# Moving a quarter-layer of key projections from one attention stage into an earlier one

## The chip, the cores and the metric

The kernel runs on one core of a Trainium2 chip. The metric is device time in microseconds (us), the median of several runs: 2410.93 us before the change (three runs, 2410.16 to 2412.91). Five engines work from queues of their own: TensorE (PE, matmuls; PEld is its loading of the stationary operand), VectorE (DVE), ScalarE (ACT), GpSimd (POOL) and SyncE (SP, which here only issues DMA transfers). Each engine takes its instructions in a fixed order and waits on semaphores.

## The reference, cut to what matters

Two transformer layers act on x of 4 batches x 512 tokens x 512 features. Every sublayer has the form `x = x + layernorm(f(layernorm(x)))`.

- Layer 0 attention: 32 heads of width 16, one shared key and value head, ALiBi bias, causal.
- Layer 0 FFN: one 512 x 512 product with dequantized weights and a bias.
- Layer 1 attention: 32 query heads of width 128, 8 key and value heads (groups g = 0..7, four query heads each), causal. Keys and values pass through a low-rank product; half of each key's coordinates are rotated by position (RoPE).
- Layer 1 FFN: a gated FFN with ternary octonion weights.

What the change touches is the key of layer 1:

```python
k_r0 = hidden_states @ Wkr.T             # the rotated coordinates
k = k * cos + _rotate_half(k) * sin
c_kv = hidden_states @ Wdk.T
k_c = c_kv @ Wupk.T                      # the other coordinates
key_full = zeros.at[..., NOPE_IDX].set(k_c).at[..., ROPE_IDX].set(k_r)
scores = jnp.einsum('bhqd,bhkd->bhqk', q, k) * scale
```

The kernel merges both key matrices into one 512 x 128 weight per group, so that the key of one (group, batch) is one product of 128 x 512 by 512 x 512, followed by a rotation whose tables are 1 and 0 on the coordinates that are not rotated.

## The kernel before

**Precision.** Matmuls run in fp32r. To keep fp32 accuracy every operand is held as a high and a low part, and a product is three matmuls per 128-wide slice of the contraction: high x high, high x low, low x high (`mm3`, and `mm3_gen`, which yields between slices). A product over 512 features takes 12 matmuls, each with a weight load of its own.

**Stages.** Layer 0 attention, and woven into it the layer 0 FFN and what layer 1 needs of x; then layer 1 attention (`phase_b`); then layer 1 FFN (class `C`).

**Layer 0 attention** is class `A1`. `run` loops over 128 steps u, one per batch, head group and block, plus 13 more to drain. In each step, four sub-steps issue the score matmuls whose row maxima DVE takes (`max_tile`, L426 and L430), and, 12 steps behind, the score matmuls whose exponentials ACT takes (`exp_tile`, L467 and L470) and the products with the values (`pv`, L483). `self.exped` counts blocks of exponentials that were issued, `self.ended` finished batches. Everything else in this stage is a Python generator in `self.gens`. `slot()` advances each of them by one yield, and it is called twice per sub-step, so eight times per step u. `hop(n)` yields n times. That is how the source order is paced; a planner in the framework, which simulates times, then sets the order on each engine.

The generators are: the query projections (`projections`), the loads of queries into QS (`loads`), the transposition of the outputs (`o_piece`) and of the maxima (`max_end`), the weight products of layer 1 (`A2.products`, which leaves the merged key weights in DRAM as `wk_d`), and two streams of posts. A post (`A2.post`) takes one tile of 128 tokens after its batch has ended: output projection, layernorm, residual, the layer 0 FFN, layernorm, residual, then the normalized x of layer 1 in transposed high and low parts. It stores these to DRAM as `xt_d` (L826) and goes on to project the values of layer 1, stored as `v_d` (L840). The last batch's four posts run side by side after the attention.

Most generators take their PSUM from the pool `mm` of two banks. A counter with two tokens (`Tok`, `self.tok`) guards it in the source: who finds no token yields and tries again.

**Layer 1 attention** is `phase_b`: 32 units u, each one group g = u // 4 and one batch b = u % 4. A unit has 16 places p (four blocks of 128 queries by four heads). While unit u computes scores, softmax, transposed probabilities, products with the values and the output projection, it also projects the queries of unit u + 1 (`qproj`, four times) and its keys (`kproj`, once, at the place j == 3 of block 0). `kproj` is 12 matmuls of 512 columns and `rope`: three DVE products out of PSUM (L859, L861, L862), a sum on POOL (L863), the rounded high part on ACT (L864) and the low part on POOL (L865); for the first unit DVE takes the place of POOL. `load_x`, `load_kv` and `load_wk` bring x, the values and the key weights from DRAM through SP's queue, x two units ahead, the values nearly one.

**Memory.** In layer 0 the key weights of layer 0 (wk_h, wk_l) are read only until the last batch's keys are projected, and the key tiles KS0 and KS1 until their batches' last exponentials; KS3 lies in another pool. The zeros that a load of QS copies came from KS0.

Of the kernel before, what the change touches and what calls it, by code (L numbers as in the profile page):

```python
# [9 lines left out]
F32 = mybir.dt.float32  # L10
# [10 lines left out]
B, S, D = 4, 512, 512  # L21
NT = B * S // 128
# [193 lines left out]
class A1:  # L216
# [40 lines left out]
    def setup(self):  # L257
        nc, aps, P = self.nc, self.aps, self.wqp
        self.wk_h = self.wp.tile([128, KC, 128], F32R, name="wk_h")
        self.wk_l = self.wp.tile([128, KC, 128], F32R, name="wk_l")  # L260
# [15 lines left out]
    def setup_consts(self):  # L276
# [4 lines left out]
        def ks(i):  # L281
            k = (self.kp if i == B - 1 else wp).tile([128, 2, 512], F32R, name=f"KS{i}")
            nc.gpsimd.memset(f(k), 0.0)
            for two in range(2):
                last = nc.gpsimd.dma_start(k[48 + 64 * two:64 + 64 * two, two], aps["c_ks"])
            self.KS.append(k)
            return last

        last = ks(0)
        with self.tc.issue_after(last.ins):  # L290
# [7 lines left out]
            self.zero = f(self.KS[0][64:68, 0, :])  # L298
# [293 lines left out]
class A2:  # L592
# [3 lines left out]
    def __init__(self, tc, nc, c, aps, a1, o_d, x2_d, xt_d, v_d, wk_d, wv_d, P):  # L596
        self.tc, self.nc, self.c, self.aps, self.a1 = tc, nc, c, aps, a1
        self.o_d, self.x2_d, self.xt_d, self.v_d = o_d, x2_d, xt_d, v_d
# [184 lines left out]
    def post(self, b, t):  # L783
# [41 lines left out]
        for i, e in enumerate((xh, xl)):  # L825
            out.dma_start(self.xt_d[i][b][:, :, bass.ts(t, 128)], f(e))  # L826
        while self.wv is None:
            yield
# [15 lines left out]

    def posts(self):

        todo = [(b, t) for b in range(B - 1) for t in range(4)]

        def stream():
            while todo:  # L850
                yield from self.post(*todo.pop(0))

        return [stream(), stream()] + [self.post(B - 1, t) for t in range(4)]
# [14 lines left out]
def phase_b(tc, nc, c, aps, xt_d, wk_d, v_d, acc, xp, P, tern, tail):  # L868

    if True:  # L870
# [43 lines left out]
        def load_kv(u):  # L914
# [6 lines left out]
            KV[u] = ts  # L921

# [7 lines left out]
        def kproj(u):  # L930
            wh, wl = W["k", u // 4]
# [96 lines left out]
        load_wk(0)  # L1028
# [4 lines left out]
        load_kv(0)  # L1033
        for j in range(4):
# [219 lines left out]
def mega(tc, nc, aps, out):  # L1254
    with ExitStack() as top:
# [16 lines left out]
        v_d = [[dp.tile([8, 128, 4, 128], F32, name=f"v{i}{b}") for b in range(B)] for i in range(2)]  # L1272
        wk_d = [dp.tile([8, 128, KC, 128], F32, name=f"wk_d{i}") for i in range(2)]
# [4 lines left out]
        with ExitStack() as e1:  # L1278
# [8 lines left out]
            a2 = A2(tc, nc, c, aps, a1, o_d, x2_d, xt_d, v_d, wk_d, wv_d, P1)  # L1287
            start = {4: [a2.weights()], 5: [a2.load_wv()], 6: a2.posts()}
            a1.run(lambda u: start.get(u, []))
        with ExitStack() as e3:  # L1290
# [4 lines left out]
            with ExitStack() as eb:  # L1295
                phase_b(tc, nc, c, aps, xt_d, wk_d, v_d, acc, xp, pools(eb), tern,
# [98 lines left out]
```

## Time and profile before

| what | value |
|---|---|
| median of three runs | 2410.93 us |
| profiled execution, whole | 2413.31 us |
| its span, first to last instruction | 2411.6 us |
| mean granted TensorE clock over the span | 0.981 |
| PE / DVE / POOL / ACT busy | 2301.8 / 1573.0 / 1190.3 / 1076.9 us |
| first and last maxima of layer 0 (L426) | 40 and 582 us |
| last exponential matmul of layer 0 (L467) | 667 us |
| first matmul of layer 1's projections | 728 us |
| last product with the values in layer 1 | 2147 us |
| DMA traffic over the span | 241.54 MB, mean 100 GB/s |

How to read it. Times in the trace count from the first instruction of the profiled execution. A group row names line, engine, operation, `out<-in` by the program's tile names, the shape and the count. A row of the timeline has start, duration, engine and line; in brackets stands the idle time before it and what ended it. A row of a table by stretch gives the stretch, its length, and for each engine the busy time and the number of instructions, then the granted TensorE clock, the mean busy share of the 16 DMA engines and the GB/s moved. Matmuls are pipelined and the ends of their records are modelled, so a busy PE is not PE at its peak: the distance between starts tells more.

### The profile page before, as it was taken

What the parts mean: (1) busy time and instruction counts of PE and PEld (TensorE: products, weight loads), DVE (VectorE), ACT (ScalarE), POOL (GpSimd) and SP (SyncE); (2) the same over time, 40 slices, a digit from 0 to 9 for tenths busy, and PEclk for the clock granted to TensorE, in tenths of its full rate; (3) what the DMA queues carried; (4) which work ended last, traced back from release to release, by engine and by line L of the source; (5) the groups of instructions that cost most, each with busy time, mean ns of one, the idle gap of its engine ahead of it and who ended that gap; (6) DMA issues with size and microseconds to landing.
All of it is one profiled execution on the core that took longest, in us unless ns stands there. A gap on an engine that the chain in (4) does not pass through costs nothing.

```text
span 2411.6 us, 35873 instructions
## 1 busy us (share of the span) xinstructions
PE 2301.8 (95%) x11606; PEld 1794.2 (74%) x11606; DVE 1573.0 (65%) x4631; ACT 1076.9 (45%) x2404; POOL 1190.3 (49%) x1387
## 2 busy tenths in 40 slices
PE   6899889988889999999999999999999999999998
PEld 4566455555557788888888888888888888878886
DVE  7766656555356777777777767777777778764443
ACT  3555445545543344444444444444444445453332
POOL 3323333434343676566566566666656667522221
PEclk8899899999999999999999999999999999999999
DMA  8845434343367432233122222232222222041000
GB/s 183 238 145 181 98 92 111 89 106 110 94 188 207 135 103 75 88 101 102 66 88 105 70 88 97 79 106 70 88 97 79 91 85 79 14 127 57 31 27 18
DMA packets 158558, 241.54 MB, mean 100 GB/s; under 512 B 26738, under 2 KB 91506, under 8 KB 149540
## 3 DMA queue, kind: packets, MB, share of 16 engines
q1 hardware_dynamic: 141748, 202.42, 27.9%
q0 software_dynamic: 14768, 35.92, 5.3%
q8 instruction: 93, 1.52, 0.3%
q10 hardware_dynamic: 1856, 0.92, 0.2%
q14 instruction: 93, 0.76, 0.1%
HBM read 183.17 MB, written 63.92 MB: 102 GB/s over the span
## 4 chain that ended last, share of the span: by engine, by line
PE 84%; issue 4%; DMA 4%; DVE 3%; POOL 2%; ACT 2%; SPq 1%; ACTq 0%; POOLq 0%; DVEq 0%
PE mm L182 11%; PE mm L184 11%; PE mm L183 11%; PE pt L989 6%; PE mm L159 3%; PE pt L467 3%; PE po L483 3%; PE po L1002 3%; PE po L1003 3%; PE mm L161 3%; PE po L1004 3%; PE mm L160 3%; PE ps L969 3%; PE ps L970 3%; PE ps L971 3%
## 5 line engine op out<-in xcount | busy, mean ns | idle before, releaser
L980 POOL TENSOR_TENSOR s<-s,r 128x384 f32<-128x384 f32 (+3 forms) x512 | 359.6, 722 | 130.0 <-DVE r L979 119.7
L977 ACT ACTIVATE s<-s,mn 128x384 f32<-128x384 f32 (+3 forms) x512 | 286.0, 560 | 223.8 <-DVE mn L973 215.9
L863 POOL TENSOR_TENSOR rp_a<-rp_a,rp_b 128x512 f32<-128x512 f32 x155 | 200.3, 1292 | 262.3 <-DVE rp_b L862 247.5
L992 ACT CAST ph<-pt 128x512 fp32r<-128x512 f32 x320 | 181.7, 586 | 295.5 <-PE pt L989 287.8
L430 DVE CUSTOM_DVE_ANT_0 jk<-ps,mask 128x384 bf16<-128x384 f32 (+3 forms) x512 | 227.5, 483 | 81.2 <-PE ps L426 72.1
L993 DVE TENSOR_TENSOR pl<-pt,ph 128x512 fp32r<-128x512 f32 x320 | 216.5, 686 | 43.4 <-ACT ph L992 40.4
L973 DVE CUSTOM_DVE_ANT_0 s<-ps,mask 128x384 f32<-128x384 f32 (+2 forms) x384 | 203.1, 552 | 37.7 <-PE ps L971 19.5
L470 ACT ACTIVATE pe<-pt 128x512 f32<-128x512 f32 x307 | 174.4, 600 | 97.0 <-PE pt L467 92.7
L989 PE MATMUL pt<-ident,s 128*128 128x128 f32 x1280 | 214.1, 272 | 0.7 <-POOL s L980 0.5
L182 PE MATMUL mm<-xh,w_h 128*128 128x512 f32 x512 | 205.4, 401 | 2.1 <-DVE rp_b L862 1.9
L182 PE MATMUL mm<-w_h,oh 128*128 128x512 f32 x512 | 203.7, 398 | 0.7 <-ACT oh L1008 0.7
L184 PE MATMUL mm<-xh,w_l 128*128 128x512 f32 x512 | 203.6, 398 | 0.0
L183 PE MATMUL mm<-xl,w_h 128*128 128x512 f32 x512 | 202.1, 395 | 0.0
L183 PE MATMUL mm<-w_l,oh 128*128 128x512 f32 x512 | 201.7, 394 | 0.0
L184 PE MATMUL mm<-w_h,ol 128*128 128x512 f32 x512 | 200.3, 391 | 0.0
L989 PEld LDWEIGHTS pt<-ident,s 128*128 128x128 f32 x1280 | 164.7, 140 | 46.1 <-POOL s L980 1.1
L865 POOL TENSOR_TENSOR ql<-rp_a,qh 128x512 fp32r<-128x512 f32 x124 | 160.5, 1294 | 49.6 <-ACT qh L864 49.6
L472 POOL TENSOR_SCALAR_AFFINE_SELECT pe<-pe 128x512 f32<-128x512 f32 x128 | 82.5, 647 | 195.7 <-ACT pe L470 195.1
L859 DVE TENSOR_TENSOR rp_a<-mm,cosq 128x512 f32<-128x512 f32 x128 | 88.4, 691 | 119.6 <-PE mm L184 94.3
L426 PE MATMUL ps<-KS,QS 128*128 128x256 f32 (+2 forms) x384 | 132.7, 384 | 19.2 <-DVE mn L430 18.7
L108 POOL TENSOR_TENSOR ln_rs<-ln_ve,mhalf 128x1 f32<-128x1 f32 x112 | 63.8, 575 | 173.0 <-DVE ln_ve L106 145.5
L1008 ACT CAST oh<-po 128x512 fp32r<-128x512 f32 x128 | 74.5, 582 | 166.1 <-PE po L1004 165.9
(359 smaller groups left out, 5872.5 us busy)
## 6 DMA issues: line engine op xcount, KB each, us to landing
xh<-xt SPq DMA_DIRECT2D x32, 1024.0 KB
xl<-xt SPq DMA_DIRECT2D x32, 1024.0 KB
vh<-v SPq DMA_DIRECT2D x32, 256.0 KB
vl<-v SPq DMA_DIRECT2D x32, 256.0 KB
raw<-in_a_wo SPq DMA_DIRECT2D x32, 256.0 KB
w_h<-in_a_wo POOLq DMA_DIRECT2D x32, 256.0 KB, 3.2
m_d<-t_d SPq DMA_DIRECT2D x192, 42.5 KB
QS<-qh_d SPq DMA_DIRECT2D x62, 128.0 KB
```

Source lines behind the costliest of these rows:

```text
L182: nc.tensor.matmul(ps, lh(k), rh(k), start=(j == 0), stop=False)
L183: nc.tensor.matmul(ps, lh(k), rl(k), start=False, stop=False)
L184: nc.tensor.matmul(ps, ll(k), rh(k), start=False, stop=(j == n - 1))
L430: nc.vector.tensor_tensor_reduce(out=jk[:, :nk], in0=p, in1=self.c.mask[:, 384 - 128 * qb:512], scale=-1.0, scalar=3e38, op0=ALU.add, op1= ...
L470: nc.scalar.activation(e, ps, AF.Exp)
L863: eng.tensor_tensor(a, a, r, ALU.add)
L973: nc.vector.tensor_tensor_reduce(out=s[:, :nk], in0=ps[:, :nk], in1=mask, scale=-1.0, scalar=3e38, op0=ALU.add, op1=ALU.min, accum_out=mn)
L977: nc.scalar.activation(s[:, :nk], s[:, :nk], AF.Exp, bias=mn, scale=-1.0, accum_out=l)
L980: nc.gpsimd.tensor_tensor(s[:, :nk], s[:, :nk], r.to_broadcast([128, nk]), ALU.mult)
L989: nc.tensor.transpose(pt[:, j], PS[u, qb, j][:, bass.ts(kb, 128)], c.ident)
L992: nc.scalar.copy(ph, pt)
L993: nc.vector.tensor_tensor(pl, pt, f(ph), ALU.subtract)
```

## The change

A new generator, `keys`, joins layer 0 attention beside the two post streams. Once 64 blocks of exponentials have been issued (so that KS0 and KS1 are done with) and all four tiles of batch 0 have stored `xt_d`, it projects and rotates layer 1's keys of batches 0 and 1, in 32 items of (batch, half of 256 tokens, group). For each half it loads x from `xt_d` into tiles of the layer 0 front (tags xn and x). For each group it loads the key weights into the tiles that held layer 0's, yields five times, takes a token, issues 12 matmuls of 256 columns (one yield after each three), rotates with three DVE products, and a POOL sum, an ACT copy and a POOL subtraction, and stores both parts to a new DRAM tensor `k_d`. The rotation tables lie in KS0's place, two output buffers in KS1's.

In layer 1, `kproj` returns at once for units of batch 0 and 1, and `load_kv` loads those units' keys from `k_d`. The key weights are still loaded for every group, since batches 2 and 3 need them; the first such load moves behind the first loads of x, tables and values. The zeros for QS come from KS3.

```diff
+    def keys(self):
+        a1, nc, c, aps = self.a1, self.nc, self.c, self.aps
+        half = lambda tag, bufs: a1.tmp.tile([128, 2, 256], F32R, name="k_x", tag=tag, bufs=bufs)
+        while a1.exped < 64 or self.split[0] < 4:
+            yield
+        tab = a1.wp.tile([128, 2, S], F32, name="k_tab", tag="KS0")
+        for i, n in enumerate(("c_cosk", "c_sink")):
+            nc.sync.dma_start(tab[:, i], aps[n])
+        out = a1.wp.tile([128, 2, 2, 256], F32R, name="k_out", tag="KS1")
+        n = 0
+        for b in range(KB):
+            while self.split[b] < 4:
+                yield
+            for hf in range(2):
+                ts = bass.ts(hf, 256)
+                x = [half("xn", 3), half("xn", 3), half("xn", 3), half("x", 2)]
+                for i, t in enumerate(x):
+                    nc.sync.dma_start(f(t), self.xt_d[i // 2][b][:, 2 * (i % 2):2 * (i % 2) + 2, ts])
+                rp = f(half("x", 2))
+                for g in range(8):
+                    w = [a1.wp.tile([128, 512], F32R, name="k_w" + e, tag="wk_" + e) for e in "hl"]
+                    for i in range(2):
+                        nc.sync.dma_start(f(w[i]), self.wk_d[i][g])
+                    yield from hop(5)
+                    yield from self.tok.take()
+                    ps = self.mmp.tile([128, 256], F32, name="mm", tag="mm")
+                    yield from mm3_gen(nc, ps, lambda k: w[0][:, bass.ts(k, 128)],
+                                       lambda k: w[1][:, bass.ts(k, 128)],
+                                       lambda k: x[k // 2][:, k % 2], lambda k: x[2 + k // 2][:, k % 2],
+                                       range(KC), hops=1)
+                    cos, sin = tab[:, 0, ts], tab[:, 1, ts]
+                    nc.vector.tensor_tensor(rp[:, 0], ps, cos, ALU.mult)
+                    yield from hop(1)
+                    nc.vector.tensor_tensor(rp[0:64, 1], ps[64:128], sin[0:64], ALU.mult)
+                    nc.vector.tensor_tensor(rp[64:128, 1], ps[0:64], sin[64:128], ALU.mult)
+                    self.tok.give()
+                    nc.gpsimd.tensor_tensor(rp[:, 0], rp[:, 0], rp[:, 1], ALU.add)
+                    yield from hop(1)
+                    o = out[:, n % 2]
+                    n += 1
+                    nc.scalar.copy(o[:, 0], rp[:, 0])
+                    nc.gpsimd.tensor_tensor(o[:, 1], rp[:, 0], f(o[:, 0]), ALU.subtract)
+                    nc.sync.dma_start(self.k_d[b][g][:, :, ts], f(o))
+                    yield
...
-        return [stream(), stream()] + [self.post(B - 1, t) for t in range(4)]
+        return [stream(), stream(), self.keys()] + [self.post(B - 1, t) for t in range(4)]
...
         def load_kv(u):
...
+            if b < KB:
+                K[u] = kvp.tile([128, 2, S], F32R, name="k", tag="k")
+                nc.sync.dma_start(f(K[u]), k_d[b][g])
...
         def kproj(u):
+            if u % 4 < KB:
+                return
...
-        load_wk(0)
         cosk, sink, cosq, sinq = (cp.tile([128, S], F32, name=n) for n in ("cosk", "sink", "cosq", "sinq"))
         load_x(0)
...
         load_kv(0)
+        load_wk(0)
...
-            self.zero = f(self.KS[0][64:68, 0, :])
+            self.zero = f(self.KS[B - 1][64:68, 0, :])
```

`KB` is 2, `self.split[b]` counts the tiles of batch b whose `xt_d` stores were issued.

More of the change, by code (lines that the diff above doesn't have):

```diff
@@ L21 @@
 B, S, D = 4, 512, 512
+KB = 2
 NT = B * S // 128
@@ L258, in setup @@
         nc, aps, P = self.nc, self.aps, self.wqp
-        self.wk_h = self.wp.tile([128, KC, 128], F32R, name="wk_h")
-        self.wk_l = self.wp.tile([128, KC, 128], F32R, name="wk_l")
+        self.wk_h = self.wp.tile([128, KC, 128], F32R, name="wk_h", tag="wk_h")
+        self.wk_l = self.wp.tile([128, KC, 128], F32R, name="wk_l", tag="wk_l")
         self.wq_h = P.tile([128, KC, 512], F32R, name="wq_h", tag="wq_h")
@@ L281, in ks @@
         def ks(i):
-            k = (self.kp if i == B - 1 else wp).tile([128, 2, 512], F32R, name=f"KS{i}")
+            k = (self.kp if i == B - 1 else wp).tile([128, 2, 512], F32R, name=f"KS{i}", tag=f"KS{i}")
             nc.gpsimd.memset(f(k), 0.0)
@@ L592, with __init__ @@
 class A2:
-    def __init__(self, tc, nc, c, aps, a1, o_d, x2_d, xt_d, v_d, wk_d, wv_d, P):
+    def __init__(self, tc, nc, c, aps, a1, o_d, x2_d, xt_d, v_d, k_d, wk_d, wv_d, P):
         self.tc, self.nc, self.c, self.aps, self.a1 = tc, nc, c, aps, a1
+        self.k_d, self.split = k_d, [0] * B
         self.o_d, self.x2_d, self.xt_d, self.v_d = o_d, x2_d, xt_d, v_d
@@ L826, in post @@
             out.dma_start(self.xt_d[i][b][:, :, bass.ts(t, 128)], f(e))
+        self.split[b] += 1
         while self.wv is None:
@@ L865, in rope, with phase_b @@
     eng.tensor_tensor(dst_l, a, f(dst_h), ALU.subtract)
-def phase_b(tc, nc, c, aps, xt_d, wk_d, v_d, acc, xp, P, tern, tail):
+def phase_b(tc, nc, c, aps, xt_d, wk_d, v_d, k_d, acc, xp, P, tern, tail):
     if True:
@@ L1272, in mega @@
         v_d = [[dp.tile([8, 128, 4, 128], F32, name=f"v{i}{b}") for b in range(B)] for i in range(2)]
+        k_d = [dp.tile([8, 128, 2, S], F32, name=f"k_d{b}") for b in range(KB)]
         wk_d = [dp.tile([8, 128, KC, 128], F32, name=f"wk_d{i}") for i in range(2)]
@@ L1286, in mega @@
                 tern.store(c)
-            a2 = A2(tc, nc, c, aps, a1, o_d, x2_d, xt_d, v_d, wk_d, wv_d, P1)
+            a2 = A2(tc, nc, c, aps, a1, o_d, x2_d, xt_d, v_d, k_d, wk_d, wv_d, P1)
             start = {4: [a2.weights()], 5: [a2.load_wv()], 6: a2.posts()}
@@ L1295, in mega @@
             with ExitStack() as eb:
-                phase_b(tc, nc, c, aps, xt_d, wk_d, v_d, acc, xp, pools(eb), tern,
+                phase_b(tc, nc, c, aps, xt_d, wk_d, v_d, k_d, acc, xp, pools(eb), tern,
                         pc.front(0))
```

## The prediction

> **What bounds the kernel now.** I read the page first: one profiled execution, 2413.3 us in all with a span of 2411.6 us, 2.4 us above the median of the runs (2410.93). TensorE (PE) is busy nearly throughout and carries 84% of the chain that ended last.
>
> ```profile
> span 2411.6 us, 35873 instructions
> PE 2301.8 (95%) x11606; PEld 1794.2 (74%) x11606; DVE 1573.0 (65%) x4631; ACT 1076.9 (45%) x2404; POOL 1190.3 (49%) x1387
> PE 84%; issue 4%; DMA 4%; DVE 3%; POOL 2%; ACT 2%; SPq 1%; ACTq 0%; POOLq 0%; DVEq 0%
> ```
>
> Busy PE hides a difference, since a matmul's recorded duration overlaps the next one's. So I read starts: in time order, PE inside layer 1 attention, with all 12 matmuls of one key projection (L182 to L184, wk_h and wk_l).
>
> ```profile
> 1107.58 0.40 PE L182 MATMUL mm<-xh,wk_h 128*128 128x512 f32 x1
> 1107.81 0.40 PE L183 MATMUL mm<-xl,wk_h 128*128 128x512 f32 x1
> 1108.05 0.39 PE L184 MATMUL mm<-xh,wk_l 128*128 128x512 f32 x1
> ...
> 1110.25 0.39 PE L184 MATMUL mm<-xh,wk_l 128*128 128x512 f32 x1
> 1110.48 0.28 PE L964 MATMUL ps<-k,qh 128*128 128x256 f32 x1
> ...
> 1110.94 0.28 PE L969 MATMUL ps<-k,qh 128*128 128x256 f32 x1
> 1111.06 0.28 PE L970 MATMUL ps<-k,qh 128*128 128x256 f32 x1
> 1111.18 0.28 PE L971 MATMUL ps<-k,ql 128*128 128x256 f32 x1
> ```
>
> Starts follow each other every 0.23 us with 512 columns and every 0.12 us with 256, though each is recorded as 0.40 and 0.28. In layer 1 there is no hole in this row of starts. In layer 0 there are many. I cut layer 0 attention where each block of eight steps u begins its maxima (every 24th matmul of L426), and took each block's busy time; the last row is one unit of layer 1.
>
> ```profile
> core 0: us, PE busy (x) PEld busy (x) DVE busy (x) ACT busy (x) POOL busy (x), PEclk, DMA share, GB/s
> 136.10:174.40 38.30, 38.16 (x212) 27.48 (x211) 21.54 (x81) 17.57 (x33) 4.63 (x8) 1.00 0.36 119
> 237.40:264.70 27.30, 21.21 (x118) 10.66 (x117) 16.50 (x70) 12.12 (x23) 10.33 (x13) 0.81 0.68 177
> 414.10:438.80 24.70, 24.70 (x152) 15.16 (x151) 17.20 (x79) 16.00 (x29) 10.37 (x16) 1.00 0.34 55
> 438.80:482.40 43.60, 38.50 (x212) 25.15 (x211) 26.56 (x104) 21.52 (x39) 18.39 (x27) 1.00 0.42 106
> 1100.00:1143.00 43.00, 43.00 (x223) 36.08 (x222) 32.34 (x89) 20.55 (x54) 30.05 (x34) 1.00 0.29 93
> ```
>
> The same attention work takes 24.7 to 43.6 us, by what the generators add beside it. The first of the three matmul lines of the layer 0 products (L159; L160 and L161 have as many) in three of these blocks:
>
> ```profile
> 136.10:174.40 38.30, 12.91 (x32) 6.01 (x32) 1.00 0.36 119
> 237.40:264.70 27.30, 0.00 (x0) 0.00 (x0) 0.81 0.68 177
> 438.80:482.40 43.60, 9.75 (x24) 4.50 (x24) 1.00 0.42 106
> ```
>
> With none, a block takes 27.3 us. With 3 x 32 projection matmuls (96 x 0.23 = 22 us) it takes 38.3: 11 us for 22, a price of 0.5 us per us of PE work. With 3 x 24 matmuls of the posts (16.6 us) it takes 43.6: 16.3 for 16.6, price 1.0. So layer 0 has some room on PE, but work put there is not free.
>
> **Removed.** 16 of 32 calls of kproj. One occupies PE from 1107.58 to 1110.48, 2.90 us, less one transposition between (about 0.1): 2.8. Sixteen make 45 us, off a stage where starts are dense. With each go three DVE products (0.69 us each), two POOL operations (1.3 each) and one ACT copy (0.62); these engines have 11 us and more free per unit (DVE 32.3 of 43), so they neither add to the gain nor become the bound at 40.2. Bounds: 45 if PE stays dense; 40 if a tenth goes back into waits. I take 45.
>
> **Added to layer 0.** 32 items (2 batches, 2 halves, 8 groups). Per item: PE 12 matmuls of 256 columns, 12 x 0.12 = 1.44 us, in all 46 us, as much as is removed. DVE three products of 256 columns at 0.42 (the 128x256 eviction at L505, also the half-partition ones, since 64x512 and 128x512 cost the same 0.69): 1.26, in all 40. POOL two at 0.61 (L980, 128x256): in all 39. ACT one at about 0.4 (L657, 128x256): 13. Where they start is set by two conditions: the batch 0 posts have stored xt (the last at 387 us) and 64 blocks of exponentials are out (397 us). An item takes 12 slots or more of the 8 that a step u has, so 16 items span 24 steps; batch 1 starts after its xt stores, the last at 532 us, and ends before or near the last exponential at 667 us. So all of it meets the maxima and the posts, apart from the last 85 us after the last maximum (582 us), where DVE is busy 27 us.
>
> I price PE's 46 us, since the other engines' work comes with it, as it does in the two blocks. Lower end 0.5, 23 us; upper end 1.0, 46 us. An item is a projection on PE but carries DVE and POOL work as a post does, so I take the middle, 0.75: 34.5 us.
>
> [...] The starts above, 0.12 against 0.23, say that the halves cost nothing extra, and I keep to them.
>
> **Edits hidden behind other work.** SP gets 2 weight loads and a store per item, 16 loads of x and two tables: 114 issues of 0.35 to 0.5 us, about 45 us, on a queue that between 400 and 660 us issues some 60. A store waits for POOL's subtraction, and behind it stand the loads of QS, which have 12 steps of slack, and the posts' v stores. If that cover went, one QS load late by a step costs 3 to 5 us. POOL's queue also issues the posts' po_ot, xr and xt transfers (landing in 2.9 to 3.1 us); each may stand behind one or two operations of 0.61, inside the waits of 10 hops that the posts have. Bytes: 16.8 MB of weights, 8.4 of stores, 4.2 of x and 0.5 of tables over 260 us add 115 GB/s to 55 to 144; the stretch 667 to 690 us ran at 226, so it fits, with longer landings. In layer 1, 16 loads of 512 KB go out with v, nearly a unit ahead; what they cost if late is bounded by their own 2.2 us at 233 GB/s each, 35 us, against nothing; I take 0. The first key comes ready instead of by kproj(0): PE waited 1.6 us twice around the first scores (L964 for qh, L182 for rp_b); bounds 0 and -3.2, I take 0, because qh is still made there. The reused SBUF (wk, KS0, KS1), load_wk(0) behind load_kv(0) and the zeros from the last KS: 0, since nothing on the chain waits for them before 728 us (the first layer 1 weights went out at 180 us, needed from 728); at most one 256 KB landing, 3 us. Clock: 414 to 482 us was granted in full, but 482 to 527 got 0.89 and 381 to 414 got 0.95; filled gaps could return up to 44.6 x 0.11 + 33.2 x 0.05 = 6.6 us. I take 0, as the keys come in bursts too.
>
> **Sum.** 2413.3 - 45 + 34.5 = 2402.8 in the profiled execution's own time; less 2.4, 2400.4 against the median. Forecast 2400, faster by 0.4%. A measurement of this kernel can tell about 0.2% (4.8 us) from no change. With price and clock at their ends this case runs from 2382 (23 us, clock returned) to 2412 (46 us).
>
> **Rivals.**
> 1. The space is really free: the keys cover only holes, as the free blocks of 24 us with 24 projection matmuls suggest (shorter than the 27.3 with none). Cost 0: 2366. Against it: PE work and block length rise together in every longer block.
> 2. The posts' price. Two tokens guard the two mm banks, and keys are a third claimant beside the two post streams. Against the 24.7 us block with 24 matmuls (5.5 us), the 43.6 us one pays 18.9 us for 11.1 more, a price of 1.7: 46 x 1.7 = 78 us, 2444. For it: the transposition of the maxima, which the exponentials need, waited 17 us after its step at 438.8 for a token. Against: keys hold a bank for about half of an item, without a layernorm in it.
> 3. The other side, by one mechanism: weights that land late in front of PE. wk_h and wk_l have one buffer each, so item g+1 loads only after g's last matmul: 1.44 for the matmuls, 0.8 for two issues, 3.1 for a landing of 256 KB, 1.1 more for the second at 233 GB/s, 6.4 us a cycle. At 24.7 us per eight steps, 12 slots come round in 4.6 us: up to 1.8 us late, and PE, in order, stands still. At half of that for all 32 items it is 29 us: 2429; at the full amount 2458. It turns the forecast to slower from 0.5 us an item ((45 - 34.5 + 4.8) / 32). Against it, layer 0 PE now loses little to DMA, since each engine's order was planned with transfer times in it:
>
> ```profile
> PE mm L147 <- ACT xn L733: 14.0, 7, 4.1
> PE pt L467 <- DMA QS<-mt: 3.6, 7, 1.1
> ```
>
> (us in total, times, longest; PE, 160 to 760 us).
>
> **How the numbers follow.** Forecast 0.45, of it 0.36 faster and 0.09 within 0.2%; rival 1 0.13 (faster); rival 2 0.14 and rival 3 0.28 (slower, but for 0.02 of rival 3 within 0.2%). Faster 0.49, same 0.11, slower 0.40. The range 2368 to 2440 leaves out half of rival 1, most of rival 2 and the upper part of rival 3, about 0.2. The likeliest case's own range is 2382 to 2412.
>
> **What would show it.** Units of layer 1: those that projected a key for batch 0 or 1 shorten from 43.5 us (the spacing of their first scores, 43.1 to 44.5) to about 40.7, the others stay; if all stay, PE was not their bound. Layer 0: the last exponential moves from 667 to about 700 us; unmoved is rival 1, past 730 rival 2 or 3. Between these, PE's waits: for DMA k_w is rival 3, bank and token waits with late mt rival 2. The prediction fails if layer 0's price lies outside 0.5 to 1.0, or if layer 1 gives back less than 40.

## The result, and the profile after

The changed kernel takes 2436.9 us (median of four runs, 2432.0 to 2441.9) against 2410.6 us before (four runs, 2408.9 to 2412.9): a ratio of 1.0107, 95% interval 1.0093 to 1.0121. It is slower by 26 us. The forecast was 2400: the sign is wrong. The time lies in the range of 2368 to 2440, but far above 2382 to 2412, the likeliest case's own.

The page of the changed kernel, profiled execution 2436.9 us: span, busy time, shares of the chain that ended last.

```profile
span 2435.2 us, 36623 instructions
PE 2310.2 (95%) x11798; PEld 1813.2 (74%) x11798; DVE 1583.1 (65%) x4677; ACT 1079.2 (44%) x2420; POOL 1198.1 (49%) x1421
PE 81%; DMA 6%; issue 5%; DVE 3%; ACT 2%; POOL 1%; SPq 1%; ACTq 0%; POOLq 0%; DVEq 0%
```

PE still carries the chain, with 3 points less; DMA has risen from 4% to 6%. That says nothing of the place, so I cut both traces at the same events: layer 0 by blocks of eight steps u, at every 24th matmul of the maxima line, as for the forecast, then at the last exponential, then by units of layer 1.

| from, to | before, us | after, us | difference | key matmuls in it (PE time) |
|---|---|---|---|---|
| start, block u72 | 340.0 | 335.0 | -5.0 | 0 |
| u72, u80 | 40.9, 33.2 | 40.9, 32.9 | -0.3 | 24 (2.8) |
| u88 | 24.7 | 42.6 | +17.9 | 48 (5.7) |
| u96 | 43.6 | 51.5 | +7.9 | 60 (7.1) |
| u104 | 44.6 | 51.7 | +7.1 | 60 (7.1) |
| u112 | 31.2 | 43.6 | +12.4 | 72 (8.5) |
| u120 | 24.2 | 38.1 | +13.9 | 36 (4.2) |
| last maximum to last exponential | 84.8 | 85.3 | +0.5 | 84 (9.9) |
| last exponential to first score of unit 8 | 432.0 | 430.0 | -2.0 | |
| unit 8 to unit 31 | 1002.3 | 971.2 | -31.1 | |
| unit 31 to the end | 310.2 | 312.3 | +2.1 | |

PE time is the number of matmuls by 0.118 us, the mean distance of the starts of a burst. The last exponential moves from 667.1 to 721.7 us. Layer 1 gives back 31.0 of those 54.6 us.

The table by stretch, for five of these blocks of after (stretch, length, busy time and instructions of PE, PEld, DVE, ACT, POOL, granted clock, DMA share, GB/s):

```profile
408.90:451.50 42.60, 37.61 (x218) 26.05 (x217) 27.06 (x102) 18.36 (x34) 17.66 (x27) 0.88 0.42 112
451.50:502.90 51.40, 44.25 (x261) 32.87 (x260) 32.07 (x110) 21.06 (x41) 22.48 (x32) 0.97 0.62 182
554.70:598.20 43.50, 36.69 (x213) 24.19 (x213) 23.69 (x89) 15.74 (x31) 15.86 (x24) 0.92 0.71 209
598.20:636.30 38.10, 34.29 (x201) 23.13 (x201) 23.13 (x92) 17.37 (x34) 16.06 (x24) 0.96 0.45 137
636.30:721.70 85.40, 74.79 (x437) 51.98 (x435) 35.52 (x90) 44.11 (x83) 45.57 (x63) 0.98 0.59 190
```

The last three of them in the trace of before:

```profile
527.00:558.20 31.20, 29.83 (x172) 18.16 (x172) 18.59 (x80) 15.25 (x29) 9.59 (x16) 1.00 0.49 144
558.20:582.40 24.20, 24.20 (x150) 14.75 (x149) 17.09 (x78) 15.67 (x28) 10.13 (x15) 1.00 0.21 67
582.40:667.10 84.70, 69.96 (x349) 43.08 (x348) 27.13 (x72) 42.70 (x77) 36.37 (x51) 0.92 0.37 122
```

The block that began at 558.20 had not a hole on PE: 24.20 of 24.20 us. Its counterpart, at 598.20, takes 38.1 us and has 3.8 idle. The blocks with little woven in (24.7, 31.2, 24.2 us) took the largest loss, 44 of 59 us, with 156 key matmuls (18.4 us); the two that hold posts (u96, u104) paid 7.9 and 7.1 for 7.1 us each, a price of 1.0 to 1.1. The tail after the last maximum, where PE was idle for 14.7 of 84.7 us, took 9.9 us of keys for 0.5. (In the other runs whose keys use a token the tail takes 80 to 97 us, so this is no exact price.)

What engines wait for, 408.9 to 636.3 us of after (us in total, times, longest):

```profile
ACT pe L471 <- PE pt L468: 62.0, 43, 5.2
POOL k_x L885 <- DVE k_x L883: 37.6, 15, 5.8
DVE k_x L880 <- PE mm L162: 27.7, 16, 4.6
PE mm L160 <- DMA k_wh<-wk_d: 3.0, 3, 1.5
PE mm L440 <- DVE k_x L883: 3.0, 2, 1.5
```

The same view of before, 414.1 to 582.4 us:

```profile
ACT pe L470 <- PE pt L467: 27.1, 32, 3.4
```

ACT waits more than twice as long for the scores that it exponentiates, while DVE and POOL stand before a key's operations, with the attention's operations behind them. PE itself waits little for the weights. One stretch shows how it goes. PE, in time order (start, duration, in brackets the idle time before and what ended it):

```profile
599.97 0.39 PE L427 MATMUL ps<-KS,QS 128*128 128x512 f32 x1
...
605.52 0.28 PE L160 MATMUL mm<-k_x,k_wh 128*128 128x256 f32 x1
605.63 0.28 PE L161 MATMUL mm<-k_x,k_wh 128*128 128x256 f32 x1
605.75 0.28 PE L162 MATMUL mm<-k_x,k_wl 128*128 128x256 f32 x1
...
609.33 0.28 PE L440 MATMUL mm<-ident,mn 128*32 128x128 f32 x1 [1.54 <-DVE k_x L883]
...
611.67 0.41 PE L423 MATMUL ps<-KS,QS 128*128 128x256 f32 x1
```

DVE, then POOL, then ACT in the same stretch:

```profile
606.76 0.70 DVE L103 BATCH_NORM_STATS2 ln_st<-mm 128x6 f32<-128x512 f32 x1 [3.02 <-PE mm L162]
607.90 0.42 DVE L880 TENSOR_TENSOR k_x<-mm,k_tab 128x256 f32<-128x256 f32 x1 [0.23 <-PE mm L162]
608.24 0.14 DVE L107 TENSOR_SCALAR ln_ve<-ln_mv 128x1 f32<-128x1 f32 x1
608.42 0.43 DVE L882 TENSOR_TENSOR k_x<-mm,k_tab 64x256 f32<-64x256 f32 x1
608.86 0.42 DVE L883 TENSOR_TENSOR k_x<-mm,k_tab 64x256 f32<-64x256 f32 x1
609.31 0.16 DVE L112 SCALAR_TENSOR_TENSOR ln_nm<-ln_mv,ln_rs 128x1 f32<-128x1 f32 x1
```

```profile
608.48 0.56 POOL L109 TENSOR_TENSOR ln_rs<-ln_ve,mhalf 128x1 f32<-128x1 f32 x1 [5.22 <-DVE ln_ve L107]
```

```profile
609.50 0.78 ACT L729 ACTIVATE x<-mm,ln_nm,ln_rs 128x512 f32<-128x512 f32 x1 [5.99 <-DVE ln_nm L112]
614.68 2.27 ACT L471 ACTIVATE pe<-pt 128x512 f32<-128x512 f32 x4 [3.96 <-PE pt L468]
```

A post and a key run together. For 11.7 us no score of the maxima starts. The key's three products (607.90 to 609.3) stand on DVE among the layernorm's operations, and ACT waits 5.99 us for the last of those, `ln_nm`. Most of that is the post's own chain: its statistics start only at 606.76, behind PE's products. The key's part in it is about 0.8 us: its first product stands before `ln_ve` (607.68, the end of the operation before, to 608.24), and `ln_rs` from POOL was ready at 609.04, 0.27 us before `ln_nm` starts. PE waits 1.54 us to transpose the maxima, because the key still holds the PSUM bank. When the next exponential comes, ACT has waited 3.96 us for it.

Layer 1 answers as forecast once it runs evenly. Four units of before, then of after:

```profile
1142.30:1316.50 174.20, 174.20 (x890) 145.69 (x889) 125.35 (x341) 79.01 (x204) 110.02 (x121) 1.00 0.26 89
```

```profile
1151.70:1320.20 168.50, 168.50 (x866) 141.15 (x865) 120.66 (x335) 78.24 (x202) 105.04 (x116) 1.00 0.29 97
```

PE is full in both, 24 matmuls are missing, and 5.7 us with them: 2.85 us a key. From unit 8 to unit 31 eleven keys are gone: 31.1 us, 2.83 each.

### The profile page after: what moved, and what is told of

The parts are those of the page before. It is cut to its first block, busy times and chain, and to the rows that moved or that the text cites. A ratio compares the mean times of both kernels' runs of the same rounds, so it can differ in the third digit from the quotient of the medians.

```text
span 2435.2 us, 36623 instructions
## 1 busy us (share of the span) xinstructions
PE 2310.2 (95%) x11798; PEld 1813.2 (74%) x11798; DVE 1583.1 (65%) x4677; ACT 1079.2 (44%) x2420; POOL 1198.1 (49%) x1421
## 3 DMA queue, kind: packets, MB, share of 16 engines
q8 instruction: 94, 1.54, 0.3%
## 4 chain that ended last, share of the span: by engine, by line
PE 81%; DMA 6%; issue 5%; DVE 3%; ACT 2%; POOL 1%; SPq 1%; ACTq 0%; POOLq 0%; DVEq 0%
PE mm L183 10%; PE mm L185 10%; PE mm L184 10%; PE pt L1043 5%; PE mm L160 3%; PE mm L162 3%; PE mm L161 3%; PE po L1056 3%; PE po L1057 3%; PE po L1058 3%; PE pt L468 3%; PE ps L1023 3%; PE ps L1024 3%; PE ps L1025 3%; PE gu L1263 3%
## 5 line engine op out<-in xcount | busy, mean ns | idle before, releaser
L912 POOL TENSOR_TENSOR rp_a<-rp_a,rp_b 128x512 f32<-128x512 f32 x140 | 180.9, 1292 | 297.5 <-DVE rp_b L911 283.8
L1027 DVE CUSTOM_DVE_ANT_0 s<-ps,mask 128x384 f32<-128x384 f32 (+2 forms) x384 | 204.1, 551 | 34.5 <-PE pt L1043 23.0
L1043 PE MATMUL pt<-ident,s 128*128 128x128 f32 x1280 | 211.7, 272 | 2.3 <-POOL s L1034 2.1
L1043 PEld LDWEIGHTS pt<-ident,s 128*128 128x128 f32 x1280 | 163.6, 140 | 46.6 <-POOL s L1034 2.8
L427 PE MATMUL ps<-KS,QS 128*128 128x256 f32 (+2 forms) x384 | 130.8, 384 | 17.2 <-DVE mn L431 16.3
L1023 PE MATMUL ps<-k,qh 128*128 128x384 f32 (+2 forms) x384 | 140.7, 366 | 5.6 <-DVE mn L1027 5.4
```

The source lines that it names most:

```text
L912: eng.tensor_tensor(a, a, r, ALU.add)
L1023: nc.tensor.matmul(ps[:, :nk], qh[:, qs], k[:, 0, :nk], start=True, stop=False)
L1027: nc.vector.tensor_tensor_reduce(out=s[:, :nk], in0=ps[:, :nk], in1=mask, scale=-1.0, scalar=3e38, op0=ALU.add, op1=ALU.min, accum_out=mn)
L1043: nc.tensor.transpose(pt[:, j], PS[u, qb, j][:, bass.ts(kb, 128)], c.ident)
```

## The experiments

**Theories.** *Sum over queues*: the price of a key in layer 0 is that of its matmuls and, on top of it, of each of its other parts, because they stand in the queues of DVE, POOL and SP in front of attention's work. *PE price*: it is PE's time alone, at a price above 0.75. *Tokens*: it is the tokens and banks that keys and posts compete for (rival 2). *Late weights*: rival 3. Where an expectation gives its theories letters or numbers, they hold for that expectation alone.

The kernels differ in when block u72 begins, before any key (332.6 to 342.5 us, and later in three with early loads). So next to the whole time I use the distance D from the start of block u72 to the last exponential, which holds all keys and none of that: 327.1 us before, 386.7 after, +59.6. That is more than the 54.6 of the last exponential, which has the earlier start of 5.0 in it. Experiments 1 to 14 are one run each, and the planner orders every kernel anew: the six kernels with no key work in that stretch (before, 1, 3, 9, 10 and 14) have D from 321.6 to 329.3. A difference of D below about 8 us is therefore not shown.

**1. Layer 1's part alone, `l1_only`**: no key is computed, and tables, x and weights are not loaded; constants are stored at the items' places. So also in 3, 9 and 10.

```diff
-                    w = [a1.wp.tile([128, 512], F32R, name="k_w" + e, tag="wk_" + e) for e in "hl"]
...
-                    nc.sync.dma_start(self.k_d[b][g][:, :, ts], f(o))
+                    yield from hop(11)
+                    nc.sync.dma_start(self.k_d[b][g][:, :, bass.ts(hf, 256)],
+                                      c.mask.rearrange("p (i t) -> p i t", i=2))
```

> Leaves out: the keys of batches 0 and 1 are not computed at all; their place in k_d is filled with 32 stores of a constant tile, at the rate of the items. Layer 1 is as in the changed kernel. All theories: layer 0 ends within 5 us of before (last exponential near 667 us), layer 1 shortens by 16 x 2.8 = 45 us, total about 2366. If it is 2380 or more, layer 1 gives back less than the row of starts says, and the loads of keys are to blame.

Measured: 2383.8 us beside 2414.8 for the kernel before, -31; D 327.6, as before. From the last exponential to the end it takes 1711.9 us against 1744.5. So layer 1 gives 31 to 33 us and not 45, with layer 0 untouched. Units 8 to 31 give 30.8, exactly eleven keys. The five keys of the first units (14 us at 2.8) give 1.5: from the last exponential to unit 8 it takes 430.5 us, against 432.0. Here is that stretch, and unit 0 within it, in the trace of before:

```profile
667.10:1099.10 432.00, 418.03 (x2077) 340.49 (x2076) 294.76 (x784) 183.00 (x445) 242.75 (x271) 0.99 0.42 124
750.60:785.70 35.10, 29.51 (x146) 23.69 (x144) 25.73 (x78) 16.53 (x45) 18.41 (x24) 1.00 0.70 187
```

In this run:

```profile
670.10:1100.60 430.50, 407.14 (x2017) 332.25 (x2016) 283.00 (x773) 182.30 (x444) 234.44 (x265) 0.98 0.42 130
753.60:787.90 34.30, 24.23 (x112) 20.09 (x111) 18.31 (x62) 12.09 (x35) 15.35 (x22) 0.85 0.71 201
```

PE has 60 matmuls less, but it is idle for 23.4 us instead of 14.0, and (1 - granted clock) sums to 10.2 us instead of 3.4. The work that is gone came back as idle time and a lower clock. PE waits for no load of a key there. What is late there, DVE and PE:

```profile
775.00 0.16 DVE L1209 TENSOR_TENSOR su<-sc 128x1 f32<-128x1 f32 x1 [12.07 <-DMA v<-x2l]
```

```profile
776.03 0.55 PE L993 MATMUL ps<-k,qh 128*128 128x256 f32 x1 [9.38 <-DVE mn L997]
```

A scalar product `su` waits for a transfer on SP's queue; with it DVE stands, and PE waits 9.4 us for a row maximum. Before, the same wait was 2.9 us, in after 6.7.

**2. That wait taken away, `after_su`**: the product is made at the start of the kernel instead.

```diff
+        nc.vector.tensor_tensor(sc[:, 3:4], sc[:, 1:2], sc[:, 2:3], ALU.mult)
...
-        su = sm.tile([128, 1], F32, name="su", bufs=1)
-        nc.vector.tensor_tensor(su, sc[:, 1:2], sc[:, 2:3], ALU.mult)
+        su = sc[:, 3:4]
```

> The whole change, with one other edit: the product of two scales that the FFN of layer 1 needs is computed at the start of the kernel, in a tile of its own, and not by DVE at the start of layer 1, where it waits until the last store of values has read the tile whose place it takes (6.7 us of DVE idle in the changed kernel, 12.1 in the run without keys, 2.9 before). If that wait is on the path: 4 to 8 us less than the changed kernel, 2428 to 2434. If something else is late there next: no change.

Measured: 2440.6 us, from the last exponential to unit 8 429.5 us. Nothing is gained. PE now waits 6.6 us for POOL at one transposition (L1043), and its idle time from the last exponential to unit 8 is 22.2 us (20.0 in after). So with that wait gone another one ends last. What sets the pace of the first units, and whether the longer wait in `l1_only` counts there, stays open.

**3. Tokens without work, `tok_only`**: as 1, and each item takes a token and holds it for five yields.

```diff
-                    yield from hop(11)
+                    yield from hop(5)
+                    yield from self.tok.take()
+                    yield from hop(5)
+                    self.tok.give()
+                    yield from hop(1)
```

> Leaves out: the keys, as in the run without them, but each item now takes a token, holds it for five yields and gives it back, with no matmul, rotation or load; constant stores stay. T4 (the shared banks set the price): layer 0 grows by 30 us or more over the run without keys, its last exponential comes at 700 us or later, total 2405 to 2420. If the price is what the keys' own instructions do to the in-order engines, the last exponential stays within 8 us of 670 us and the total within 2380 to 2392.

Measured: 2373.5 us, D 321.6. The token as a third claimant costs nothing here; the token theory falls in this form.

**4. Keys in other banks, `no_tok`**: the keys' PSUM comes from the attention's pool psS, without a token.

```diff
-                    yield from self.tok.take()
-                    ps = self.mmp.tile([128, 256], F32, name="mm", tag="mm")
+                    ps = a1.psS.tile([128, 512], F32, name="ps", tag="ps")[:, :256]
...
-                    self.tok.give()
```

> The whole change, but the keys' matmuls write to the pool of three banks that the maxima use, without a token. T4: the added time of layer 0 falls from 55 to 35 us or less, total 2405 to 2418. Otherwise it stays at 50 or more, or grows, since the maxima have one bank less: 2430 to 2450.

Measured: 2425.0 us, 12 less than after; D 378.3. The keys now begin in block u72 and end before the last maximum; that block takes 49.7 us instead of 40.9 and u80 46.6 instead of 32.9, and the tail 62.8 instead of 85.3. The price wanders to where the keys go. At most about 8 of the 60 us are the banks', no more than the scatter of D.

**5. A quarter of the matmuls, `few_mm`**: 3 of 12, the rest of the item as it is (the keys are partial sums).

```diff
-                                       range(KC), hops=1)
+                                       range(1), hops=1)
+                    yield from hop(3)
```

> Leaves out: 9 of the 12 matmuls of each item (the other three slices of the contraction), with the same number of yields; loads, rotation and stores stay. T1: PE work goes from 45 to 11 us, so the added time of layer 0 falls to a quarter, 14 us: total 2390 to 2395. T3 and T4: the rotation and the bank's holding stay, 2415 to 2435.

Measured: 2416.7 us, D 374.6: 12.1 us for 34.5 us of PE work taken away, 0.35 per us. The PE price falls: at 0.75 or more, 26 us or more would be gone. Block u88, whose keys are down to 12 matmuls, 1.4 us:

```profile
409.00:444.40 35.40, 30.34 (x173) 19.84 (x173) 23.39 (x93) 15.91 (x30) 15.28 (x22) 0.90 0.46 124
```

It takes 35.4 us against 24.7 before, with 5 us of PE idle where there was none. Some of its length comes with 10 post matmuls (2.3 us) that have moved in from the block before; the rest is waiting.

**6. No rotation, `act_evict`**: one ACT copy out of PSUM replaces three DVE products, two POOL operations and the copy (the keys stay unrotated, the low part is not made).

```diff
-                    nc.vector.tensor_tensor(rp[:, 0], ps, cos, ALU.mult)
...
-                    nc.scalar.copy(o[:, 0], rp[:, 0])
-                    nc.gpsimd.tensor_tensor(o[:, 1], rp[:, 0], f(o[:, 0]), ALU.subtract)
-                    nc.sync.dma_start(self.k_d[b][g][:, :, ts], f(o))
+                    nc.scalar.copy(o[:, 0], ps)
+                    self.tok.give()
+                    yield from hop(1)
+                    for i in range(2):
+                        nc.sync.dma_start(self.k_d[b][g][:, i, ts], f(o[:, 0]))
```

> Leaves out: the rotation. One ACT copy of 256 columns evicts the bank in place of three DVE products, two POOL operations and the copy; matmuls, loads and bytes stay. T3: most of the added time goes, total 2385 to 2400. T1: stays, 2425 to 2440. T4: a part goes, since the bank comes free a little earlier, 2415 to 2430.

Measured: 2420.3 us, D 373.2: the rotation costs 13.5 us.

**7. Weights once for eight groups, `no_wload`** (the other seven are computed with the first group's weights).

```diff
-                    w = [a1.wp.tile([128, 512], F32R, name="k_w" + e, tag="wk_" + e) for e in "hl"]
-                    for i in range(2):
-                        nc.sync.dma_start(f(w[i]), self.wk_d[i][g])
+                    if g == 0:
+                        w = [a1.wp.tile([128, 512], F32R, name="k_w" + e, tag="wk_" + e) for e in "hl"]
+                        for i in range(2):
+                            nc.sync.dma_start(f(w[i]), self.wk_d[i][g])
```

> Leaves out: the key weights are loaded for the first group of each half alone (8 loads instead of 64), so seven of eight keys are wrong. Theory T2 (late weights and DMA traffic, rival 3): most of the added 55 to 60 us of layer 0 goes, total 2385 to 2400. Theories T1 (PE work), T3 (DVE and POOL standing behind a key's matmuls) and T4 (the two mm banks): little changes, 2425 to 2440.

Measured: 2422.3 us, D 369.2: the weight loads cost 17.5 us, though PE waits for them only 5.3 us in 408.9 to 721.7. DVE's wait for the key's last matmul shows more. PE's wait for the low part (the high part's stands above) and DVE's in after over that stretch, then DVE's in this run from 408.9 to 705.1:

```profile
PE mm L162 <- DMA k_wl<-wk_d: 2.3, 4, 0.8
DVE k_x L880 <- PE mm L162: 31.0, 21, 4.6
```

```profile
DVE k_x L881 <- PE mm L162: 15.7, 18, 3.7
```

The wait passes on to the engine that stands in front of the late product.

**8. Both away, `mm_only`**: edits 6 and 7 together.

> Leaves out: both the rotation (one ACT copy evicts) and seven of eight weight loads; all 384 matmuls, tokens, loads of x and stores stay. If the price is a sum over the parts of an item (so far 11 us for nine of twelve matmuls, 13 for the rotation, 17 for the weight loads, of some 55), the last exponential comes at 721.7 - 13 - 17 = 692 us, total about 2405. If the parts are one chain of which any one left in place keeps the price, it stays at 705 or later, total 2418 or more. If only the two together matter, it falls below 680, total below 2395.

Measured: 2408.1 us beside 2411.3; D 354.6. This closes the sum. From `l1_only` (327.6) to `mm_only` (354.6) the matmuls, x loads, a copy and stores cost 27.0; to `act_evict` (373.2) the weights 18.6 more; to after (386.7) the rotation 13.5. By the other way, over `no_wload` (369.2), it is 27.0, 14.6 for the rotation, 17.5 for the weights. Weights and rotation add up within 1.1 us either way, as the sum over queues says. The matmuls by themselves have a price of at most 27.0 / 46 = 0.59 per us, since x loads, copy and stores are in the 27.0; `few_mm` gave 0.35. Both lie below the 0.75 of the forecast.

**9. Weights' bytes without a reader, `loads_only`**: as 1, and each item loads its weights, which nobody reads.

```diff
+                    w = [a1.wp.tile([128, 512], F32R, name="k_w" + e, tag="wk_" + e) for e in "hl"]
+                    for i in range(2):
+                        nc.sync.dma_start(f(w[i]), self.wk_d[i][g])
                     yield from hop(11)
```

> Leaves out: matmuls, rotation, tokens and loads of x; the weight loads (16.8 MB through SP, each pair into the same two buffers) and the constant stores stay. No engine waits for these loads. If traffic and SP's queue alone set the 17 us of the weight loads, the last exponential comes at 680 to 690 us against 661 to 670 without them, total 2385 to 2400. If it was the waiting of engines for late weights, it stays at 661 to 672, total 2372 to 2385.

Measured: 2413.2 us, 29 more than `l1_only`, but not where it was meant: with nothing to wait for, the planner put the loads at 191 to 336 us, and block u72 begins at 370.9 instead of 342.5; D is 329.3, no cost at all. **10. Tied to an exponential, `loads_timed`** (`with self.tc.issue_after(a1.last_exp.ins):` around the loads):

> The kernel without the keys (constant stores, 2383.8 us, last exponential at 670.1), plus the 64 weight loads that nobody reads, each pair tied to the exponential that was last given out, so that they run at the items' own times (from about 400 us) and not early as in the run with untied loads. Theory A (the 17 us that the weights cost are bytes and SyncE's queue: 16.8 MB more, and 64 more issues ahead of QS): last exponential 680 to 687, whole kernel 2394 to 2401, QS waits on TensorE and DMA share above those of the run without loads. Theory B (the weights cost because TensorE, in order, stands before a matmul whose weights are late, and with it all behind): 669 to 673, 2382 to 2387.

Measured: 2400.0 us, u72 at 358.1, D 328.8: the loads ran at 186 to 325 us again. **11. The same behind 8, `mm_loads`**:

```diff
+                    d = a1.wp.tile([128, 2, 512], F32, name="k_dummy", tag="KS0")
+                    with self.tc.issue_after(a1.last_exp.ins):
+                        for i in range(2):
+                            nc.sync.dma_start(d[:, i], self.wk_d[i][g])
```

> The kernel with the keys' matmuls and one ACT copy but no rotation and a weight load for the first of eight items only (2408.1 us, last exponential 695.8), plus the other loads' bytes into a tile that nobody reads, tied to the exponential last given out. The same kernel with real weight loads had 708.4 and 2420.3. Theory A (bytes and queue): back to 704 to 712 and 2416 to 2424. Theory B (late weights before an in-order TensorE): stays at 693 to 699 and 2405 to 2411.

Measured: 2432.7 us, over the upper end; the loads ran at 250 to 392 us, and D rose by 17.2 to 371.8: 11.0 in the two blocks with loads (u72 48.3, u80 41.1), 5.5 in the tail, little between. In those two blocks, SP's waits and then PE's:

```profile
SPq L873 <- DMA k_dummy<-wk_d: 26.8, 10, 5.2
```

```profile
PE pt L468 <- DMA QS<-mt: 8.2, 1, 8.2
```

SP stands before a load whose buffer is still being filled, and PE waits 8.2 us for QS. The trace follows that one back: the transfer PE needed was issued by ACT at 367.22 us, released by a QS load of SP that landed at 367.20; SP had issued that one at 361.32, behind waits for `k_dummy` that ended at 353.75 and 357.22. So SP's queue entered it, and so did a landing of 5.9 us. None of the three is the clean test of the bytes at the items' time, but all three lost 16 to 29 us of whole time to loads that nobody read.

**12 and 13. The clean test, `mm_touch` and `mm_tied`**: a one-element ACT copy after each eviction holds the tile (in the place of the rotation's tables, which are not loaded here). The last two lines are in the second run alone.

```diff
                     nc.scalar.copy(o[:, 0], ps)
+                    d = a1.wp.tile([128, 2, 512], F32, name="k_dummy", tag="KS0")
+                    nc.scalar.copy(d[0:1, 0, 0:1], f(o[0:1, 0, 0:1]))
+                    for i in range(2):
+                        nc.sync.dma_start(d[:, i], self.wk_d[i][g])
```

> Control for the next run: the kernel with the keys' matmuls and one ACT copy, no rotation, weights loaded for the first of eight items only (2408.1 us, last exponential 695.8), plus one ACT copy of a single element per item into an unread tile. 32 copies of about 0.2 us on an engine that is busy 44%: last exponential 694 to 703, whole kernel 2406 to 2415, by either theory.

> As the control, and behind each one-element copy two 256 KB weight loads on SyncE into the same unread tile: the copy comes after the item's eviction, so each pair starts when the real loads would, and no matmul waits for them. Theory A (bytes, 64 issues and SyncE's queue are what the weights cost): last exponential 10 to 16 us after the control's. Theory B (the cost is TensorE, in order, and behind it DVE, before products whose weights are late): within 4 us of the control.

Measured: control 2411.6 us, D 355.5; with loads, all but one issued from 395 to 675 us as they should be, 2418.7 and 362.4. Last exponential +6.6, between the two theories; D +6.9. With real weights (`act_evict`) D is 373.2, 10.8 more. So of about 18 us that the weights cost, 7 would be bytes and SP's queue, and 11 come with the matmuls' need of them; the 7 lie within the scatter of D, the 11 a little beyond it. In the copies' wait it shows; control, loads unread, loads read (400 us to the last exponential or nearly):

```profile
ACT k_out L880 <- PE mm L162: 27.4, 22, 4.2
```

```profile
ACT k_out L880 <- PE mm L162: 27.6, 18, 4.2
```

```profile
ACT k_out L882 <- PE mm L162: 47.8, 24, 5.9
```

**14. All keys after the maxima, `late128`.**

```diff
-        while a1.exped < 64 or self.split[0] < 4:
+        while a1.u < 128 or a1.exped < 64 or self.split[0] < 4:
```

> The whole change, but the keys start only at step 128, after the last maximum, so that they lie in the last 12 steps and beside the last batch's posts. In the changed kernel the blocks with maxima grew by 59 us while the stretch after them kept its 85 us with 10 us of key matmuls in it. If the price is set by the collision with the maxima, the cost falls to 15 to 35 us, total 2385 to 2410. If it is set by the work wherever it lies, the total stays at 2425 to 2445.

Measured: 2527.1 us, above the ranges of both theories. The last exponential is early (659.6), but unit 1 begins at 937.4: the keys outlast the tail. Waits from 640 to 940 us, and two stretches (columns as above):

```profile
DVE k_x L880 <- PE mm L162: 98.9, 24, 11.9
PE mm L160 <- DMA k_wh<-wk_d: 76.7, 22, 10.0
```

```profile
760.00:820.00 60.00, 36.08 (x161) 29.81 (x160) 15.55 (x34) 8.35 (x16) 16.96 (x23) 0.73 0.90 261
820.00:880.00 60.00, 28.42 (x111) 24.63 (x111) 11.43 (x27) 3.64 (x9) 15.01 (x20) 0.56 0.61 181
```

Here rival 3 is seen in full, 3.5 us at 22 of the loads. In these two stretches PE is busy for 36.08 and 28.42 of 60 us, the granted clock is 0.73 and 0.56, and the DMA engines' share is 0.90 and then 0.61.

**15 and 16. Half the keys, `kb1`, and spread out, `kb1_paced`.**

```diff
-KB = 2
+KB = 1
```

> The change for batch 0 alone (KB = 1): half of the items, all between steps 76 and about 104. Layer 1 gives back 8 x 2.8 = 22 us. If the price is even over the items, layer 0 pays half of 55, 27 us: total 2412 to 2422, the same as before or slightly slower. If the items beside the posts cost less than those in the free blocks (batch 0's blocks grew by 33 us, batch 1's by 26): up to 2425.

Measured, four runs: 2439.3 us, ratio 1.0111 (1.0094 to 1.0128), as slow as with two batches. D is 365.6, +38.5 for half the items: the same blocks as in after (u88 +18.2, u96 +7.7, u104 +7.4), and later only the tail, +4.3, though no key lies in it. So the price is not even over the items. And layer 1 gives 6.0 us from unit 8 to 31, where five keys would be 14; the units become uneven (units 7 to 10: 40.9, 43.5, 45.6, 43.1 against 43.6, 43.1, 44.0, 43.5), and PE's start distances show the rest as small delays scattered over many lines; their cause stays open. The paced version has 19 slots an item instead of 12:

```diff
-                    yield from hop(5)
+                    yield from hop(8)
                     yield from self.tok.take()
...
+                    yield from hop(3)
                     cos, sin = tab[:, 0, ts], tab[:, 1, ts]
...
                     self.tok.give()
+                    yield from hop(2)
                     nc.gpsimd.tensor_tensor(rp[:, 0], rp[:, 0], rp[:, 1], ALU.add)
                     yield from hop(1)
+                    yield from hop(1)
...
                     nc.scalar.copy(o[:, 0], rp[:, 0])
+                    yield from hop(1)
```

> As the run with one batch, but each item is stretched from 12 slots to 19: eight yields instead of five after the weight loads, three more before the first DVE product, three more before the POOL sum and the ACT copy, one more before the POOL subtraction. Nothing is left out. If the price lies in queue heads that stand waiting (DVE stood idle 33 us before key instructions, POOL 68, ACT 15, PE 10), layer 0 pays 10 to 15 us instead of 27: total 2398 to 2406, faster than before. If it is the work itself, the total is that of the run with one batch, within 4 us.

Measured, four runs: 2434.0 us, ratio 1.0087 (1.0071 to 1.0102); D 361.9. Block u88 takes 36.6 us instead of 42.9, u96 61.9 instead of 51.3, u104 38.9 instead of 52.0, u120 32.9 instead of 24.1. Pacing in the source moves the price, and takes 4 to 5 us of it.

No version with all of the computation beats the kernel before.

## Why the prediction was wrong, point by point

**Removed: 2.8 us a key, right; 45 us in all, wrong.** In the even part of layer 1 a key is worth 2.83 us. The lower bound, "40 if a tenth goes back into waits", was too high: layer 1 gave 31.0 back in after and 32.6 in `l1_only`. The missing 12 to 14 us are the five keys of the first units. I had read a dense row at 1107 to 1111 us and carried it over to units 0 to 7. Before, PE has 14.0 us of idle time ahead of unit 8, nearly all of it up to the end of unit 0; with the keys gone it has 20 to 23, and a lower clock (0.98 on average against 0.99). There PE was not the only bound. This is 14 of the 34 us between 2402.8 and 2436.9; the other 20 are layer 0's.

**Added: 34.5 us forecast, 54.6 measured (59.6 from u72 on).** This is the failed step, and within it two terms. Per us of PE work the keys paid 1.2 to 1.3, above the bound of 1.0. The price was not too low for PE's own work: the matmuls with little beside them cost 27.0 us, 0.59 per us, and by `few_mm` 0.35. "I price PE's 46 us, since the other engines' work comes with it" is what failed: the rotation on DVE and POOL cost 13.5 to 14.6 us more. In the two blocks from which the price came, that work was part of other jobs. And "edits hidden behind other work", SP's 64 weight loads put at 0, cost 17.5 to 18.6: some 7 by bytes and SP's queue, about 11 only where the matmuls use the weights. The named cover, QS loads with 12 steps of slack and a late one at 3 to 5 us, went once: PE waits 4.5 us for one of them, far below that price. That the parts cost this much the runs show; that they do it by standing in front of other work is seen in single stretches, and how much of each goes that way is not shown.

**Where: one price for all blocks.** The sum had the same price everywhere, and rival 1 took the free blocks for room, since they were short. They were short and full, PE 24.70 of 24.70 us, a line that the forecast shows. They paid 44 us for 18.4 us of keys and about 3 us net of post matmuls that moved in. The base of the price was misread as well: the block of 27.3 us without layer 0 products has PE busy for 21.21 us at a granted clock of 0.81, so its length is not what the attention needs. Against the block of 24.7 us, with 5.5 us of post matmuls, the same two blocks pay 13.6 us for 16.5 and 18.9 for 11.1: 0.8 and 1.7, not 0.5 and 1.0. Of room that I put in no sum there was one place, the tail, where 9.9 us of keys cost 0.5.

**Rival 1** (free space, 2366) falls but for the tail. **Rival 2** (2444): near in time, wrong in mechanism: tokens cost nothing, other banks take at most 8 us off. Its price of 1.7, formed on a free block, came nearest to what free blocks paid. **Rival 3** (late weights, 2429 to 2458): part of it, 0.35 us an item (11 / 32), below its turning point of 0.5; with the forecast's other terms it alone would not have made the kernel slower. Waits of PE for the weights are only 5.3 us. **Clock**: (1 - granted), summed from 378 us on to the last exponential, is 13.7 us before and 18.8 after; `act_evict` has 11.9 and is still long, so it is not the cause. **Range:** that 2437 lies in it owes to the shares of rivals 2 and 3, which are not what happened; that is luck.

**Matmuls of 256 columns.** The starts of 0.12 us held in the bursts of after (605.52, 605.63 and 605.75 in the stretch shown), and the matmuls' price came out below 0.75: no run shows an extra cost of the halves.

**One order of the queues was left out.** In the stretch shown, `ln_nm` starts on DVE at 609.31, right behind the key's last product (608.86, 0.42 us), though its operand from POOL was ready at 609.04, 0.27 us before. I had asked what stands behind the new work for PE, in rival 3, and for the transfers on SP and POOL, but not for the layernorms and maxima on DVE, ACT and POOL.

## What to carry to other kernels

A short stretch isn't a free one: look whether its bounding engine has holes before giving it work, and take a stretch with holes (here the tail after the last maximum) first, as far as it reaches: all keys together outlast it (experiment 14). Price moved work by all the queues that it enters, each with a term of its own; in a coupled stage rotation and weights each cost 13 to 19 us and added up, though no engine but PE was near full. And a rate read in the even part of a loop doesn't hold for its first turns: of 16 keys taken out the first 5 gave next to nothing.

## What the runs showed of the hardware

64 loads of 256 KB that no instruction reads cost 16 to 29 us of whole time (0.25 to 0.46 us each) where they went through SP's queue at 186 to 392 us of layer 0 (experiments 9 to 11, one run each). In after, an issue of the key weights on SP took 0.32 to 0.56 us for the high part (median 0.33) and 0.33 to 0.82 for the low part (median 0.38). In `late128`, 22 waits of PE for one weight load add up to 76.7 us from 640 to 940 us, the longest 10.0. In the two stretches of that run shown above, the DMA share is 0.90 and 0.61, and the granted clock 0.73 and 0.56 with PE busy for 60% and 47% of the time.
